# Two stacked cross-attention models: the order of five engines written out by a clock kept while the program is traced

## The chip, the cores and the metric

The kernel runs on one core of one Trainium2 chip. The metric is device time in microseconds (us) of one launch. The kernel before took 2897.28 us, the median of 3 runs (2894.77 to 2900.27).

## The reference

Inputs are `x` and `ctx`, both 16 sequences of 256 tokens of 512 channels, and a mask of 16x256x256. Two model blocks follow each other. In short:

```python
# block 0
q = layer_norm(x) @ q_w;  k, v = split(layer_norm(ctx) @ kv_w)     # 16 heads of 32
x = x + softmax(where(mask, -max, q k^T / sqrt(32))) v @ proj_w + proj_b
x = x + gelu(layer_norm(x) @ fc1_w + fc1_b) @ fc2_w + fc2_b        # 512 -> 2048 -> 512
# block 1, with m = (row of x is not all zero)
x = ln1(x + mha(x, x, Wq1, Wk1, Wv1, m, causal=True))
m = (row of x is not all zero)
x = ln2(x + mha(x, ctx, Wq2, Wk2, Wv2, m, causal=False))
x = ln3(x + (relu(x @ fc1 + b1) @ fc2 + b2) * m)
# mha multiplies Q, K, V and its output by m, counts the non-zero energies of
# query 0 per head ("lengths"), and masks the keys beyond that count
```

Everything is float32. A product is made of three passes of a reduced float32 type: each operand is split into a high part and a low remainder, and high*high, high*low and low*high are added.

## The kernel before

The 16 sequences are handled in 8 groups of two (512 tokens, four tiles of 128 rows, `G = 4`). There are four stages:

1. Block 0's attention, a group at a time (8 groups).
2. Block 0's MLP (`Mlp0.run`), 8 groups of 16 hidden chunks, `up` and `down` alternating.
3. Block 1: 8 self-attention groups, then 8 cross-attention groups (`block1`, the jobs `Mha`).
4. Block 1's MLP (`mlp_feed`), 8 groups.

In the attention stages two generators are interleaved by `weave`. The main one, `Attention.stream`, goes through heads (32 to a group): `scores` (two matmuls on TensorE into one of two `sc` banks of PSUM, the row maximum on VectorE, two exponentials on ScalarE with their sums), three heads later `turn` (transposes of the exponentials into a `pt` bank, and a copy of it to SBUF on ScalarE), and for every eight heads `mix` and `finish`. The other, `feed(g)`, makes the next group's operands meanwhile: it transposes the rows (`transposed`), projects Q, K and V (12 passes of 512 columns for each of 4 chunks), splits each product into its high and low part (`split`: ScalarE makes the high part, VectorE the low), and in block 0 adds the output projection (`residual`). The parts of Q and K go through DRAM (`keep`) and come back as `stack` tiles, three of which exist; `build` loads one for every four heads, with four or five DMAs.

In block 1, `front(n + 1, t)` transposes tile `t` of the next group's rows, and tests them with `nonzero`: a pass over the row on VectorE, whose result is `m`. The rows come by `rows_in`, one DMA into one of three `x` tiles, called when the third Q chunk of group `n` has been projected. That tile is free once `norm` of group `n-2` has stored its rows.

Weights are loaded in rows of 128x512 by `Weight.load`: a DMA, the high part, the low part. In attention they use the nine buffers `pts` that also hold the transposed exponentials; in `Mlp0` four buffers in turn.

The order within an engine is set in two ways. TensorE takes the order in which the program is traced:

```python
    with tc.manual_schedule(engines={mybir.EngineType.PE}):
        block1(phase1())
```

VectorE, ScalarE, GpSimdE and the queue of SyncE, which issues every DMA, are ordered by a planner, which lays out a timeline of its own and may put any instruction that it holds for ready ahead of others. Work of which the tracer knows that it isn't ready is deferred by counting heads: `Attention.later` holds closures, of which one is run after each head.

Of the kernel before, what the change touches and what calls it, by code (L numbers as in the profile page):

```python
# [10 lines left out]
F32 = mybir.dt.float32  # L11
# [9 lines left out]
P = 128  # L21
# [16 lines left out]
PASS = 216.0  # L38
# [5 lines left out]
def kernel(ctx: ExitStack, tc: tile.TileContext, a, out):  # L44

# [58 lines left out]

    def rows(ap):
        return ap.rearrange("(t p) c -> p t c", p=P)
# [16 lines left out]
    def split(src, dst, bias=None, scale=None):  # L123

        if bias is not None:
            nc.scalar.activation(dst[0], src, AF.Identity, bias=bias)
            nc.vector.scalar_tensor_tensor(
                dst[1], src, bias, dst[0].bitcast(F32), ALU.add, ALU.subtract
            )
        elif scale is not None:  # L130
            nc.scalar.activation(dst[0], src, AF.Copy, scale=scale)
            nc.vector.scalar_tensor_tensor(
                dst[1], src, scale, dst[0].bitcast(F32), ALU.mult, ALU.subtract
            )
        else:
            nc.scalar.copy(dst[0], src)
            nc.vector.tensor_tensor(dst[1], src, dst[0].bitcast(F32), ALU.subtract)
# [5 lines left out]
    class Weight:  # L143
# [4 lines left out]
        def __init__(  # L148
            self,
            pool,  # L150
            stage,
# [11 lines left out]
            self.stage = stage  # L163
# [4 lines left out]
            self.form, self.raw = form, {}  # L168
# [8 lines left out]
        def load(self, ks, x0=0, n=C):  # L177

            at = slice(x0, x0 + n)
            for k in ks:  # L180
                h, l = (self.reorder(w[:, k, at]) for w in self.w)
                raw = self.stage()
                nc.sync.dma_start(
                    out=raw, in_=a[self.name][ts(k, P), self.c0 + x0 : self.c0 + x0 + n]
                )
                raw = self.raw[k] = self.order(raw)
                if self.gain is None:
                    nc.scalar.copy(h, raw)
                    nc.gpsimd.tensor_tensor(out=l, in0=raw, in1=h.bitcast(F32), op=ALU.subtract)
                elif self.form is None:  # L190
                    by = self.gain[:, k : k + 1]
                    nc.gpsimd.tensor_scalar(raw, raw, by, None, ALU.mult)
                    nc.vector.tensor_copy(h, raw)
                    nc.gpsimd.tensor_tensor(out=l, in0=raw, in1=h.bitcast(F32), op=ALU.subtract)
                else:
                    by = self.gain[:, k : k + 1]
                    nc.scalar.activation(h, raw, AF.Identity, scale=by)
                    parts = [(l, raw, h)]
                    if self.heads:
                        parts = [(l[:, c], raw[:, c], h[:, c]) for c in range(n // P)]  # L200
                    for to, of, less in parts:
                        nc.vector.scalar_tensor_tensor(
                            to, of, by, less.bitcast(F32), ALU.mult, ALU.subtract
                        )
        def weigh(self, pool):

            self.by_k = None
            for k, raw in self.raw.items():
                self.by_k = weigh(pool, self.by_k, raw, self.offset[:, k : k + 1], self.reorder)

        def shift(self):
# [4 lines left out]
            else:  # L216
                sum_cols(self.b, by_k)

    def load_weight(*args, **kwargs):
        w = Weight(*args, **kwargs)  # L220
        w.load(range(KC))
        return w
# [11 lines left out]
    def sum_cols(b, by_k, first=True):  # L234

        ps = bank("mm", "ps_b")
# [8 lines left out]
    def ln_stats(pool, src):  # L245

        st = pool.tile([P, nc.vector.BN_STATS_DIM], F32, tag="bnst", name="st")
        mv = pool.tile([P, nc.vector.BN_AGGR_DIM], F32, tag="bnmv", name="mv", bufs=4)
        nc.vector.bn_stats(st, src)  # L249
        nc.vector.bn_aggr(mv, st)  # L250
        rstd = pool.tile([P, 2], F32, tag="bnrs", name="rstd", bufs=4)
# [4 lines left out]
    def normalize(pool, dst, src):  # L256
        mean, rstd = ln_stats(pool, src)
        nc.vector.tensor_scalar(dst, src, mean, rstd, ALU.subtract, ALU.mult)

    def layer_norm(pool, x, gain, offset, pooled=False):  # L260
        mean, rstd = ln_stats(pool, x)
        if pooled:
            nc.vector.tensor_scalar(x, x, mean, rstd, ALU.subtract, ALU.mult)
            nc.gpsimd.tensor_tensor(out=x, in0=x, in1=gain, op=ALU.mult)
            nc.gpsimd.tensor_tensor(out=x, in0=x, in1=offset, op=ALU.add)
        else:
            nc.vector.scalar_tensor_tensor(x, x, mean, gain, ALU.subtract, ALU.mult)
            nc.vector.scalar_tensor_tensor(x, x, rstd, offset, ALU.mult, ALU.add)
# [18 lines left out]
    def transposed(dst, src, t, tag="mm"):  # L287
# [4 lines left out]
        split(ps, (dst[0][:, :, ts(t, P)], dst[1][:, :, ts(t, P)]))  # L292
# [55 lines left out]
    def weave(main, n_main, fill, n_fill):  # L348
        a = f = 0.0
        main_on = fill_on = True  # L350
        while main_on or fill_on:
            if fill_on and (not main_on or f * n_main < a * n_fill):
# [5 lines left out]
                if cost is not None:  # L358
                    f += cost
                    continue  # L360
                assert main_on
# [7 lines left out]
            else:  # L369
                a += cost  # L370


    class Attention:
# [8 lines left out]
        def __init__(self, pool, scratch, n, biased):  # L382
# [7 lines left out]
            self.n_build = 0  # L390
            self.later = []
# [948 lines left out]
```

## Time and profile before

| | us |
|---|---|
| median of 3 runs | 2897.28 |
| profiled execution, its own time | 2894.72 |
| its span, first to last instruction | 2892.9 |
| TensorE busy | 2722.3 (94% of the span) |
| VectorE, ScalarE, GpSimdE busy | 1713.3, 1624.5, 777.2 |

So 1.8 us of the profiled execution lie outside its span, and it stands 2.6 us under the median.

The stages, cut in the timeline at the first scores of the groups named. "Clock" is the mean clock that TensorE was granted, as a share of the full one:

| stretch, us from the start | what | length | TensorE busy | VectorE | ScalarE | clock |
|---|---|---|---|---|---|---|
| 0 to 69.4 | group 0's operands, no attention | 69.4 | 43.1 | 52.0 | 36.1 | 0.98 |
| 69.4 to 152.5 | block 0, group 0 | 83.1 | 75.8 | 50.3 | 62.0 | 0.98 |
| 324.3 to 408.0 | block 0, group 3 | 83.7 | 82.0 | 53.1 | 61.3 | 1.00 |
| 652.0 to 730.7 | block 0, last group, and the loading of `fc1_w` | 78.7 | 69.1 | 55.6 | 57.6 | 0.91 |
| 730.7 to 1462.6 | MLP of block 0 | 731.9 | 721.0 | 246.3 | 120.3 | 1.00 |
| 1462.6 to 1501.2 | block 1, group 0's operands | 38.6 | 33.7 | 31.4 | 14.1 | 0.96 |
| 1709.0 to 1781.2 | block 1, a self-attention group | 72.2 | 66.3 | 51.2 | 52.8 | 0.95 |
| 2000.0 to 2079.6 | the last self group, first cross weights | 79.6 | 70.6 | 55.9 | 61.7 | 0.96 |
| 2396.9 to 2476.4 | block 1, a cross-attention group | 79.5 | 73.6 | 52.3 | 59.5 | 0.98 |
| 2636.2 to 2892.9 | last cross group, MLP of block 1 | 256.7 | 237.9 | 188.9 | 112.0 | 0.98 |

The profile's busy time of TensorE counts the modelled tail of a matmul, so a busy TensorE is not one at its peak; how dense the matmuls lie is read from the distance of their starts.

### The profile page before, as it was taken

The page shows a single profiled execution, that of the slowest core. Times are in us where ns is not written, and L with a number is a line of the kernel's source. Part 1 is how long each engine was busy: PE and PEld are TensorE (multiplying, and loading weights), DVE is VectorE, ACT ScalarE, POOL GpSimd, SP SyncE. Part 2 cuts the span into 40 slices and gives each one's busy share as a digit, 9 for nine tenths or more (in the row PEclk, how much of TensorE's full clock was granted, in tenths as well). Part 3 has the DMA queues.
Part 4 walks back from the last instruction along what each step waited for, and adds up shares of the span by engine and source line. Part 5 has one row for each costly group of instructions (what it writes and reads, how often), then busy time and mean ns, then how long its engine had stood idle before and what let it go on. Part 6 is the DMA issues. An engine that isn't in the chain of part 4 may idle for free.

```text
span 2892.9 us, 49424 instructions
## 1 busy us (share of the span) xinstructions
PE 2722.3 (94%) x16698; PEld 2202.6 (76%) x16698; DVE 1713.3 (59%) x5151; ACT 1624.5 (56%) x4732; POOL 777.2 (27%) x714
## 2 busy tenths in 40 slices
PE   6999999998999999999999999998999999998998
PEld 4777778786888888888878777776777777777777
DVE  7666666657533223332267677666766666666777
ACT  5777777777221111111147777777777777777532
POOL 5222212216621001110022222224323332333433
PEclk9999999999999999999999999999999999999999
DMA  7666656656310000000065565556665555654221
GB/s 224 182 170 191 185 167 188 194 168 161 91 44 30 15 15 30 30 30 0 30 212 166 176 176 176 176 176 212 187 194 178 180 169 175 184 179 141 81 102 59
DMA packets 230299, 393.60 MB, mean 136 GB/s; under 512 B 27936, under 2 KB 126752, under 8 KB 230048
## 3 DMA queue, kind: packets, MB, share of 16 engines
q1 hardware_dynamic: 230048, 390.45, 45.0%
q8 instruction: 134, 2.20, 0.3%
q14 instruction: 117, 0.96, 0.1%
HBM read 247.22 MB, written 143.13 MB: 135 GB/s over the span
## 4 chain that ended last, share of the span: by engine, by line
PE 69%; DVE 11%; DMA 10%; ACT 3%; POOL 2%; issue 2%; SPq 1%; POOLq 0%; DVEq 0%; ACTq 0%
PE ps_p L274 26%; PE acc L274 12%; PE ps_v L274 12%; PE ps_pt L465 7%; PE ps_z L482 5%; PE ps_s L424 4%; DMA x<-xd 4%; PE ps_t L291 2%; ACT e L449 2%; DVE e L439 2%; DMA xd<-x 2%; DVE st L249 1%; DVE mn L435 1%; DMA xin<-in_ctx_dram 1%; DVE junk L941 1%
## 5 line engine op out<-in xcount | busy, mean ns | idle before, releaser
L449 ACT ACTIVATE e<-e,mn 128x256 f32<-128x256 f32 (+1 forms) x1024 | 487.3, 480 | 119.0 <-DVE mn L439 115.0
L468 ACT COPY pt<-ps_pt 128x512 f32<-128x512 f32 (+1 forms) x768 | 417.9, 552 | 102.5 <-PE ps_pt L465 98.7
L465 PE MATMUL ps_pt<-ident,e 128*128 128x128 f32 x2816 | 447.7, 278 | 21.5 <-ACT pt L468 19.9
L424 PE MATMUL ps_s<-stack 97*128 97x256 f32 (+1 forms) x1536 | 335.0, 300 | 86.9 <-DVE mn L439 44.3
L875 ACT ACTIVATE hg<-ps_p,b_fc 128x512 f32<-128x512 f32 x128 | 88.1, 688 | 580.5 <-PE ps_p L274 550.0
L465 PEld LDWEIGHTS ps_pt<-ident,e 128*128 128x128 f32 x2816 | 342.1, 143 | 71.9 <-ACT pt L468 34.3
L424 PEld LDWEIGHTS ps_s<-stack 97*128 97x128 f32 (+1 forms) x1536 | 276.1, 193 | 157.2 <-ACT e L449 56.4
L274 PE MATMUL acc<-fc_w_h,hid 128*128 128x512 f32 x1024 | 337.6, 392 | 0.0
L274 PE MATMUL ps_p<-x_t,fc_w_h 128*128 128x512 f32 x1024 | 317.0, 390 | 0.0
L140 DVE CAST hid<-hg 128x512 fp32r<-128x512 f32 x128 | 62.9, 491 | 386.5 <-ACT hg L875 386.4
L253 POOL TENSOR_TENSOR rstd<-rstd,nhalf 128x1 f32<-128x1 f32 x192 | 125.1, 657 | 572.8 <-DVE rstd L252 540.6
L449 ACT ACTIVATE e<-ps_s,mn 128x256 f32<-128x256 f32 x512 | 243.7, 495 | 33.3 <-DVE mn L435 30.7
L439 DVE CUSTOM_DVE_ANT_0 e<-mb,ps_s 128x256 f32<-128x256 bf16 x512 | 190.7, 412 | 73.9 <-PE ps_s L424 70.8
L435 DVE TENSOR_REDUCE mn<-ps_s 128x2 f32<-128x512 f32 x256 | 174.6, 682 | 99.7 <-PE ps_s L424 96.2
L274 PEld LDWEIGHTS acc<-fc_w_h,hid 128*128 128x128 f32 x1024 | 192.3, 188 | 42.2
L274 PEld LDWEIGHTS ps_p<-x_t,fc_w_h 128*128 128x128 f32 x1024 | 192.3, 188 | 42.0
L274 PE MATMUL ps_p<-x_t,q_h 128*128 128x512 f32 x640 | 212.4, 413 | 0.0
L1041 POOL TENSOR_TENSOR x<-x,zz 128x512 f32<-128x512 f32 x64 | 83.6, 1306 | 467.3 <-DVE zz L1034 327.7
L439 DVE CUSTOM_DVE_ANT_0 e<-tri,ps_s 128x128 f32<-128x128 f32 (+1 forms) x512 | 159.9, 345 | 75.7 <-PE ps_s L424 70.7
L274 PE MATMUL ps_p<-x_t,fc_w_l 128*128 128x512 f32 x512 | 201.1, 393 | 0.0
L274 PE MATMUL acc<-fc_w_l,hid 128*128 128x512 f32 x512 | 200.5, 392 | 0.0
L449 ACT ACTIVATION_READ_ACCUMULATOR e<-e,mn 128x1 f32 x1024 | 197.2, 193 | 0.0
(178 smaller groups left out, 5794.6 us busy)
## 6 DMA issues: line engine op xcount, KB each, us to landing
d<-qk SPq DMA_DIRECT2D x192, 512.0 KB
stack<-d SPq DMA_DIRECT2D x384, 256.0 KB
stack<-d SPq DMA_DIRECT2D x384, 128.0 KB
xd<-x SPq DMA_DIRECT2D x96, 256.0 KB
x<-xd SPq DMA_DIRECT2D x24, 1024.0 KB
wst<-in_fc_w_dram SPq DMA_DIRECT2D x48, 256.0 KB
xin<-in_ctx_dram SPq DMA_DIRECT2D x32, 256.0 KB
xr<-in_x_dram SPq DMA_DIRECT2D x32, 256.0 KB
```

Of the source, the lines that this page charges most:

```text
L140: nc.vector.tensor_copy(dst[0], src)
L253: nc.gpsimd.tensor_tensor(out=rstd[:, 1:2], in0=rstd[:, 0:1], in1=nhalf, op=ALU.pow)
L274: nc.tensor.matmul(ps, w[p], x[q], start=(k == 0 and i == 0), stop=(k == kc - 1 and i == 2))
L424: nc.tensor.matmul(ps[:, t, :], st[: self.rows, 0, j % HPC, ts(t, P)], st[: self.rows, 1, j % HPC, :], start=True, stop=True,)
L435: nc.vector.tensor_reduce(mn, ps, AX.X, ALU.min)
L439: nc.vector.tensor_tensor_reduce(out=e[:, at], in0=bias[t], in1=ps[:, t, : job.width[t]], scale=-SC, scalar=BIG, op0=ALU.add, op1=ALU.min, ...
L449: nc.scalar.activation(e[:, at], ps[:, t, :] if bias is None else e[:, at], AF.Exp, bias=mn[:, t : t + 1], scale=-1.0, accum_out=u.rs[:, t ...
L465: nc.tensor.transpose(pp[:, ts(x, P)], e[:, at : at + P], ident)
L468: nc.scalar.copy(pt[:, :n], pp[:, :n])
L482: nc.tensor.matmul(z[ts(j, D), c * S + w[0] * P : (c + 1) * S], job.v[u.i * NT + mc][:, at : at + D], u.pt[c * HPC + j][:, x0 * P : (x0 + ...
L875: nc.scalar.activation(hg, ps, AF.Gelu, bias=b_fc1[:, k : k + 1], scale=1.0)
L1041: nc.gpsimd.tensor_tensor(out=xv, in0=xv, in1=zz, op=ALU.add)
```

## The change

All five engines take the order of the trace (`tc.manual_schedule()` without a list), so no planner moves anything. For that the tracer keeps a clock: `weave` advances it by the price of each traced product (`tick`), and `after(ns, do)` defers a piece of work by that many ns of it. `step_on` runs the next deferred piece at once, `settle` all that are left, and `Loader.ensure(n)` as many as it takes until n weight rows are in.

With that clock, work is placed as follows.

- `split`, `normalize`, `norm`, `residual`, `lengths`, `keep` and the stores: each step that waits for another engine is traced 0.8 to 6 us after it.
- `scores` is divided; the exponentials of head n are traced behind the `turn` of head n-3.
- `build` is called up to two stacks ahead, on heads that don't begin a stack; where none is there when the head needs it, it is called at that head.
- `shared`: in block 0's last group the copy of every second head's transposes goes from ScalarE to VectorE; in cross-attention that of every fourth.
- `nonzero` is a maximum of absolute values and a comparison. It is made where the rows are produced (`Mlp0.out`, and `norm` once stored), not where they are read back.
- `rows_in` (through `next_rows`) comes after the fourth Q chunk, once `norm` of group n-2 has been traced.
- `Loader` replaces `Weight.load`: four rows ahead in block 0, two buffers for `fc1_w`, one buffer (`wst`) for `fc2_w` and for all weights of block 1. Of `fc1_w` ScalarE makes every high part; the low part is VectorE's for even rows, and two GpSimdE instructions for odd ones.
- In `Mlp0` the next group's rows come by one DMA instead of four and are normalized in hidden chunks 5 to 11; their four normalized tiles have a buffer each.
- Pacing prices change (`PASS` 216 to 230 ns, `mix` 1950 to 2100).

The core of the diff:

```diff
+    def after(ns, do, lasting=False):
+        heapq.heappush(due, (now[0] + ns, next(number), lasting, do))
+    def tick(ns):
+        end = now[0] + ns
+        while due and due[0][0] <= end:
+            at, _, _, do = heapq.heappop(due)
+            now[0] = max(now[0], at)
+            do()
+        now[0] = end
...
-    def split(src, dst, bias=None, scale=None):
+    def split(src, dst, bias=None, scale=None, lag=800.0, then=None):
...
+        if lag:
+            after(lag, rest)
...
+    class Loader:
+        def pump(self):
+            while self.queue and self.flying < self.ahead:
+                w, k, x0, then = self.queue.pop(0)
+                raw = self.stage()
+                w.fetch(raw, k, x0)
+                self.flying += 1
+                self.last = max(self.last + self.gap, now[0] + self.wait)
+                after(
+                    self.last - now[0],
+                    lambda w=w, raw=raw, k=k, x0=x0, then=then: self.split(w, raw, k, x0, then),
+                    True,
+                )
+        def split(self, w, raw, k, x0, then):
+            w.use(raw, k, x0)
+            after(750.0, self.landed, True)
+        def ensure(self, n):
+            while self.done < n:
+                step_on()
...
     def stream(self, jobs):
...
                     if j % HPC == 0:
-                        u = units[un]
-                        u.st[j // HPC] = self.build(u.job, u.i, u.c + j // HPC)
-                    self.scores(units[un], j)
-                    yield 2 * 110.0
+                        while n_built <= m:
+                            assert self.build(n_built, jobs)
+                            n_built += 1
+                        u.st[j // HPC] = self.stacks.pop(m)
+                    self.scores(u, j)
+                    if (
+                        n_built <= min(m + len(self.tiles) - 1, len(heads) // HPC - 1)
+                        and n % HPC
+                        and self.build(n_built, jobs)
+                    ):
+                        n_built += 1
+                    yield 2 * 119.0
                 if LAG <= n < len(heads) + LAG:
                     un, j = heads[n - LAG]
                     yield self.turn(units[un], j)
+                if n < len(heads):
+                    self.exponentials(*((units[heads[n][0]], heads[n][1])))
...
-                if self.later:
-                    self.later.pop(0)()
...
     def last():
             yield from more_values(NG - 1)
+            settle()
...
+            mlp.load_up()
...
         def load_up(self):
+            self.up_loader = Loader(self.stage, 2, 3500.0, 1600.0)
             for x0 in range(0, HID, C):
                 for k in range(KC):
-                    self.fc1.load([k], x0)
-                    yield 2 * PASS
+                    self.up_loader.ask(self.fc1, k, x0)
...
     def run(self, early, following, after_up):
+            loader = self.loader = Loader(
+                lambda: pool.tile([P, C], F32, tag="wst", name="wst", bufs=1), 1, 3000.0, 1400.0
+            )
+            for k in range(self.NH):
+                loader.ask(self.fc2, k)
...
     def nonzero(pool, src, m):
-        junk = pool.tile([P, C], F32, tag="t512", name="junk", bufs=3)
-        nc.vector.tensor_scalar(
-            junk, src, 0.0, None, ALU.not_equal, ALU.max, accum_out=m
-        )
+        top = pool.tile([P, 1], F32, tag="top", name="top", bufs=1)
+        nc.vector.tensor_reduce(top, src, AX.X, ALU.max, apply_absolute_value=True)
+        nc.vector.tensor_scalar(m, top, 0.0, None, ALU.not_equal)
...
     def norm(self, t):
+                def stored():
+                    nc.sync.dma_start(
+                        out=xd[3 if self.cross else 2][self.g][ts(t, P), :], in_=x
+                    )
+                    if not self.cross:
+                        nonzero(pool, x, m1[:, self.g, t : t + 1])
+                    self.stored += 1
...
     def front(n, t):
-            cost = transposed(job.x_t, x, t)
-            if n:
-                nonzero(pool, x, job.m[:, t : t + 1])
-            return cost
+            return transposed(job.x_t, x, t, "mm" if t or n else "z")
...
     def feed(n):
-                if c == 2:
-                    next_rows(n)
+            while n >= 2 and jobs[n - 2].stored < G:
+                yield None
+            next_rows(n)
...
-    with tc.manual_schedule(engines={mybir.EngineType.PE}):
+    with tc.manual_schedule():
```

## The prediction

> **What bounds the kernel now.** I read the page's busy shares first, then the waits of TensorE, the timeline about the longest of them, and the chain for the pace of matmuls.
>
> ```profile
> PE 2722.3 (94%) x16698; PEld 2202.6 (76%) x16698; DVE 1713.3 (59%) x5151; ACT 1624.5 (56%) x4732; POOL 777.2 (27%) x714
> ...
> PE ps_s L424 <- DVE mn L439: 44.3, 17, 5.9
> PE ps_s L424 <- ACT e L449: 33.5, 21, 4.6
> ...
> DVE junk L941 <- DMA x<-xd: 46.8, 13, 6.1
> ```
>
> TensorE is the bound, and no other engine is near 94%. It idles 171 us in all. Its longest waits (total, times, longest) are for a row maximum or an exponential, because there are two `sc` banks. The third line says why those are late: VectorE itself stood 13 times, 46.8 us, before `nonzero` (`junk`) for rows still on their way. The timeline of a self-attention group:
>
> ```profile
> 1594.49 0.37 SPq L1062 DMA_DIRECT2D x<-xd  x1
> ...
> 1601.94 0.69 DVE L941 TENSOR_SCALAR_CACHE_REDUCE junk<-x 128x512 f32<-128x512 f32 x1 [5.62 <-DMA x<-xd]
> ...
> 1604.26 0.40 ACT L449 ACTIVATE e<-e,mn 128x128 f32<-128x128 f32 x1 [5.05 <-DVE mn L439]
> ...
> 1604.66 0.76 PE L424 MATMUL ps_s<-stack 97*128 97x256 f32 x2 [5.43 <-DVE mn L439]
> ```
>
> The rows are asked for at 1594.49; VectorE, in order, is stuck behind the test until 1601.94, then does the tests, and the scores wait 5.43 us. This comes once in each later group of block 1.
>
> How dense can it be? The chain (start, length, what) gives 12 passes of 512 columns; the timeline of block 0, two scores and four transposes, by the distance of starts:
>
> ```profile
> 852.71 2.75 PE acc L274 x12
> ...
> 442.54 0.40 PE L424 MATMUL ps_s<-stack 96*128 96x256 f32 x2
> 442.78 0.60 PE L465 MATMUL ps_pt<-ident,e 128*128 128x128 f32 x4
> 443.13 0.71 PE L274 MATMUL ps_p<-x_t,q_w_h 128*128 128x512 f32 x2
> ```
>
> So 0.23 us a pass, 0.12 a score, 0.09 a transpose; a `mix` is 1.6 by the same reading. A self group is 144 passes (33.1), 64 scores (7.7), 96+32 transposes (11.3), 4 mixes (6.4) and 16 matmuls of `lengths` (1.9): 60.3 us, where 72.2 are spent. A cross group is 66.0 against 79.5, a full block 0 group 75.5 against 83.7. Of the 11.9 us of the self group 5.9 are idle (72.2 less 66.3) and 3.6 are the clock (0.95 granted); 2.4 are seams between unlike matmuls, which stay. Of the cross group's 13.5: 5.9 idle, 1.6 clock, 6 seams. Block 0 loses 1.7 idle of its 8.
>
> **What the Trainium skill says.** "TensorE: Matmul & The Clock Gate", Part 1: about 3.4 us of idleness halve the clock until it has been busy as long. The trace agrees: 0.50 from 1605 to 1609 us, after the 5.43 us gap. A stall costs more than itself. "PSUM — Partial Sum Buffer", Engine vs sequencer instructions: ScalarE's, VectorE's and GpSimdE's queues are strict FIFO; the stall above is that. [...]A quiet load here took 2.68 (`wst`, issued 812.51, read 815.19); in attention 3 to 6. "SBUF — State Buffer", two separate sides: a VectorE instruction of two SBUF inputs and GpSimdE exclude each other. The low part of `hid` took 0.69 alone and 1.66 beside GpSimdE: agrees, and no forecast rests on more.
>
> **The change, part by part.** In the instruction order of the changed kernel TensorE has the same 15,135 instructions, SyncE 24 fewer, VectorE 136 more, ScalarE 64 fewer. So no product gets cheaper; all depends on waits.
>
> *Tests and rows, block 1.* Removed are 64 tests of 0.68+0.08; added are 64 maxima (nearest row: `mn` of 128x512, 0.68) and comparisons (nearest 0.13): +3 us of VectorE, beside other work, as VectorE has 21 us free in a self group. They now read rows in SBUF and wait for no load. Bounds: -10 to +15 us. Gone is the 5.4 us gap with its half clock. Late next is TensorE itself: its first transposes of the rows. By the order, 5.7 us of TensorE work lie between the load's issue and them in self groups, 8.8 in cross groups; the load takes 6.6 to 7.5 us (self) and 6.0 to 6.6 (cross) in the chain. So 1.3 us come back per self group, none in cross. Six self groups regain 5.9+3.6-1.3 = 8.2, less 1 for a lost head or so (ScalarE has 19 us free, in order): **-43**. Six cross groups: 5.9+1.6-1 = 6.5: **-39**. The two at the seam of self and cross idle 9.0 and 5.0; new loads (below) use half: **-8**.
>
> *`shared`.* 80 copies of 0.57 go from ScalarE to VectorE (nearest 0.68): both keep over a quarter free. Nothing; without that cover at most 0.1 a head.
>
> *One-buffer loaders.* A row's cycle is load, ScalarE's high part, GpSimdE's low part, next issue. For `fc2_w`: 2.7+0.6+1.45+0.2 = 4.9 us, where the clock grants 3.75. Sixteen rows in ScalarE's queue fall behind the order by 1.15 each; behind row 14 stands gelu 11, and behind that `down` and TensorE. Of 16 us two chunks of slack (11) absorb most: +8 (0 to 16). For block 1 the cycle is 4.3+1.2+1.6+0.3 = 7.4 against 4.75, so each set of four rows blocks ScalarE 3 x 2.6 = 8 us, of which perhaps 3 are absorbed. Sets k1, v1 at block 1's start: +8; q2, k2, v2: in the seam's -8; f1, f2: +7. The first stacks of each attention have nothing ahead of them: `build` issues four DMAs of 0.5 when the first scores are next, and these land 4 to 5 us later: +6 in block 0, +6 in block 1.
>
> *`fc1_w`.* The odd rows share one buffer: 3.0 (load) + 0.6 + 1.56+1.29 (GpSimdE) + 0.4 = 6.9 us each; seven intervals take 48 us, where the order puts 25 us of TensorE's work. ScalarE, and SyncE with the stacks behind it, wait. 55 of dense work and 2 of seams become 80, against 78.7 now, since GpSimdE's two steps for all 16 rows (3 us each) pace it already: +2 (-12 to +12).
>
> *Start.* TensorE idles 26 us of the first 69.4: 7.5 before the first tile, 6.4 before the second, whose normalization stood behind other tiles. Tile after tile costs about 3.2 us of VectorE and ScalarE; I take **-11** (-18 to 0).
>
> *Block 0.* Row loads have 4 to 5 us of work ahead of them, where 23 waits for them stalled VectorE 40 us. Against that five heads run without passes beside them, while `residual` waits for `done`; they were three: ScalarE needs 1.7 a head, TensorE 0.6, so +1.5 a group. Net **-9** (-20 to +5).
>
> *MLP of block 0.* The fronts' waits (0.37 and 1.11 at seven groups) go, as the tiles are ready four chunks early: -10. *MLP of block 1:* the load of the next rows stands in SyncE's queue behind the last output store of the group before, and has 6 us for 5 to 6: +3 (0 to 10).
>
> Sum: -43-39-8-11-9-10+8+8+7+6+6+2+3 = **-80**, and -20 for the short waits elsewhere (33 us of excess in the last stretch, 16 in block 0's first group): **-100**. 2894.7-100 = 2794.7; the median stands 2.6 above: I say 2796.
>
> **Rivals.** *All is regained*: loads land early enough for ScalarE never to meet one unlanded. Then the loaders' +23 and half the +12 fall away, and cross and self lose nothing: 2740. For it: quiet loads of 2.7 us. Against: one buffer.
> *The wait changes its owner*: TensorE stands for the rows itself as long as VectorE did. Then only half of 82 in block 1 comes: 2840. For it: 5.7 against 7 us.
> *ScalarE becomes the bound, slower.* Place: the self and cross groups. Strict trace order puts head n's exponentials behind head n-3's copy, and that behind TensorE. In a dense self group ScalarE has (65-52.8)/32 = 0.38 us a head to wait in, in a cross group (72.5-57)/32 = 0.48. Each 0.1 beyond costs 0.1 x 32 x 16 = 51 us. From about 0.65 a head it eats the 100. At 0.75 the time is 2960. For it: no planner fills a gap. Against: `turn` precedes scores whose exponentials are due 4.4 us later (two banks).
> *The change doesn't do what it says*: the order shows that it does, on every engine.
>
> **How the numbers follow.** Likeliest 2796, its own range 2745 to 2835, chance 0.55; all regained 0.13; owner changed 0.15; no change to speak of 0.03; slower 0.14. 0.2% is 6 us, about what a measurement can tell. Faster 0.83. Range 2735 to 2875, which leaves out the slower case and a little below.
>
> **What would show it.** Right: no VectorE wait for `x<-xd` in block 1, self groups of 64 to 66 us and cross of 72 to 74 at a clock of 1.00, ScalarE waiting for `wst`, TensorE once for `stack` at each start. Wrong: self groups at 72 with ScalarE or TensorE waiting elsewhere, or the `fc1_w` stretch over 95.

## The result, and the profile after

The changed kernel took 3013.91 us, the median of 4 runs (3007.41 to 3017.12), against 2896.52 us for the kernel before: 1.040 of its time, 95% interval 1.038 to 1.042. The forecast was 2796 us (2735 to 2875), with a chance of 0.14 for slower. The profiled execution spans 3015.3 us, 122.4 more than before.

The page and the waits of TensorE (in all, times, longest, in us) of the changed kernel:

```profile
PE 2769.2 (92%) x16698; PEld 2219.0 (74%) x16698; DVE 1831.7 (61%) x5223; ACT 1589.0 (53%) x4668; POOL 744.4 (25%) x698
```

```profile
PE ps_s L517 <- ACT e L547: 52.0, 69, 3.2
PE ps_t L374 <- DMA x<-xd: 25.2, 8, 12.3
...
PE ps_s L517 <- DMA stack<-d: 14.8, 2, 9.0
...
PE ps_t L374 <- DVE wst L346: 9.5, 1, 9.5
PE ps_p L357 <- DVE tok L1131: 7.9, 1, 7.9
```

VectorE no longer waits for `x<-xd` anywhere, as forecast. But TensorE, still the busiest engine at 92%, now idles 246 us instead of 171, for many different things: rows, stacks, a normalized tile, the first-token row. It is also busy 47 us longer with the same products. The clock that it was granted is 0.970 on the mean, where it was 0.981; by an estimate from these two figures that is 35 us of the 122.

Cut at the first scores of each group, as in the table of before, the time went here (lengths in us; the last two columns are experiments told below):

| stretch | before | forecast, as a difference | after | difference | `planner4` | `before_tests` |
|---|---|---|---|---|---|---|
| start | 69.4 | -5 | 93.5 | +24.1 | 77.6 | 69.4 |
| block 0, first seven groups | 582.7 | -9 | 599.2 | +16.5 | 576.7 | 578.6 |
| last group and `fc1_w` | 78.7 | +2 | 94.8 | +16.1 | 79.8 | 76.6 |
| MLP of block 0 | 731.9 | -2 | 729.6 | -2.3 | 742.9 | 732.5 |
| block 1: operands and first group | 101.1 | +14 | 118.9 | +17.8 | 107.3 | 109.6 |
| six self groups | 436.3 | -43 | 420.2 | -16.1 | 411.8 | 416.2 |
| seam, two groups | 157.0 | -8 | 155.6 | -1.4 | 148.7 | 148.7 |
| six cross groups | 479.2 | -32 | 497.0 | +17.8 | 466.6 | 450.0 |
| last cross group, MLP of block 1 | 256.8 | +3 | 306.5 | +49.7 | 268.2 | 256.5 |

(The -20 that the forecast gave to "short waits elsewhere" belongs to no row.) A steady self group and a steady cross group of the kernel after, by windows (length, then busy time and instructions of TensorE, its weight loads, VectorE, ScalarE and GpSimdE, then TensorE's clock, DMA share and GB/s):

```profile
1704.30:1772.40 68.10, 64.92 (x481) 53.33 (x480) 52.50 (x219) 51.48 (x181) 17.62 (x17) 1.00 0.63 187
...
2374.60:2456.60 82.00, 75.89 (x528) 59.47 (x528) 57.22 (x128) 55.76 (x177) 23.91 (x20) 0.98 0.57 170
```

The self group has its clock back (1.00, 0.95 before) and is 4 us shorter. The cross group is longer than before (79.5), with the same work on TensorE.

Where a cross group waits, the timeline shows. Each line: start, length, engine and line; in brackets the idle time before it and what ended it.

```profile
2475.14 0.68 DVE L174 SCALAR_TENSOR_TENSOR qk<-ps_p,qk 128x512 fp32r<-128x512 f32 x1
...
2475.44 0.51 PE L517 MATMUL ps_s<-stack 97*128 97x256 f32 x2
2475.74 0.68 DVE L176 TENSOR_TENSOR c_t<-ps_t,c_t 128x512 fp32r<-128x512 f32 x1
...
2476.34 0.68 DVE L335 BATCH_NORM_STATS2 st<-x 128x6 f32<-128x512 f32 x1
...
2477.34 0.68 DVE L528 TENSOR_REDUCE mn<-ps_s 128x2 f32<-128x512 f32 x1
...
2478.12 0.47 ACT L547 ACTIVATE e<-ps_s,mn 128x256 f32<-128x256 f32 x1 [2.25 <-DVE mn L528]
...
2479.19 0.80 PE L517 MATMUL ps_s<-stack 97*128 97x256 f32 x2 [2.10 <-ACT e L547]
```

The scores of 2475.44 are done by 2475.95, but their row maximum starts at 2477.34: VectorE has two low parts and the statistics of a norm ahead of it, which the clock of traced products placed there. ScalarE waits 2.25 us for that maximum, and TensorE 2.10 us for ScalarE to free a bank. The same wait of 2.1 us stands in each of the six cross groups of the table.

In the MLP of block 1 a group takes 30.3 us (fronts at 2875.15 and 2905.41), where its 96 passes and 16 transposes are 23.5 at the forecast's prices and a group of the kernel before took 24.2:

```profile
2823.65 0.74 DVE L1482 SCALAR_TENSOR_TENSOR x<-x,mv,ln 128x512 f32<-128x512 f32 x1
2823.73 1.82 POOL L1473 TENSOR_TENSOR x<-x,y 128x512 f32<-128x512 f32 x1
...
2824.49 1.60 DVE L1485 SCALAR_TENSOR_TENSOR x<-x,rstd,ln 128x512 f32<-128x512 f32 x1
...
2826.12 14.52 SPq L1486 DMA_DIRECT2D out_dram<-x  x4
...
2840.75 0.38 SPq L1453 DMA_DIRECT2D x<-xd  x1
2846.27 0.63 PE L374 MATMUL ps_t<-ident,x 128*128 128x128 f32 x4 [1.73 <-DMA x<-xd]
```

VectorE's last pass over a tile takes 1.60 us, beside GpSimdE's addition of 1.82. The four output stores leave SyncE between 2826.12 and 2840.6, each when VectorE is done with its tile, and the load of the next rows stands behind the last of them. It is issued at 2840.75, lands 5.5 us later, and TensorE has waited 1.73 us.

### The profile page after: what moved, and what is told of

Its sections match the earlier page's. It is cut to its first block, busy times and chain, and to the rows that moved or that the text cites. A ratio compares the mean times of both kernels' runs of the same rounds, so it can differ in the third digit from the quotient of the medians.

```text
span 3015.3 us, 49215 instructions
## 1 busy us (share of the span) xinstructions
PE 2769.2 (92%) x16698; PEld 2219.0 (74%) x16698; DVE 1831.7 (61%) x5223; ACT 1589.0 (53%) x4668; POOL 744.4 (25%) x698
## 4 chain that ended last, share of the span: by engine, by line
PE 62%; DVE 17%; DMA 6%; ACT 6%; issue 4%; POOL 4%; SPq 0%; POOLq 0%; DVEq 0%; ACTq 0%
PE ps_p L357 23%; PE acc L357 11%; PE ps_v L357 10%; PE ps_pt L562 6%; PE ps_z L583 4%; PE ps_s L517 4%; DMA wst<-in_fc_w_dram 3%; ACT e L547 3%; PE ps_t L374 2%; DVE st L335 2%; DMA x<-xd 2%; DVE mn L528 2%; DVE x L1485 1%; DVE e L531 1%; DVE x_t L176 1%
## 5 line engine op out<-in xcount | busy, mean ns | idle before, releaser
L547 ACT ACTIVATE e<-e,mn 128x256 f32<-128x256 f32 (+1 forms) x1024 | 487.4, 481 | 77.3 <-DVE mn L531 76.5
L569 ACT COPY pt<-ps_pt 128x512 f32<-128x512 f32 (+1 forms) x688 | 372.2, 541 | 157.2 <-PE ps_pt L562 156.2
L339 POOL TENSOR_TENSOR rstd<-rstd,nhalf 128x1 f32<-128x1 f32 x192 | 113.4, 591 | 953.8 <-DVE rstd L338 940.8
L357 PE MATMUL ps_p<-x_t,q_h 128*128 128x512 f32 x640 | 219.1, 422 | 15.5 <-DVE tok L1131 7.9
```

The lines of the kernel that those rows point to most:

```text
L339: nc.gpsimd.tensor_tensor(out=rstd[:, 1:2], in0=rstd[:, 0:1], in1=nhalf, op=ALU.pow)
L357: nc.tensor.matmul(ps, w[p], x[q], start=(k == 0 and i == 0), stop=(k == kc - 1 and i == 2))
L547: nc.scalar.activation(e[:, at], e[:, at] if ps is None else ps[:, t, :], AF.Exp, bias=mn[:, t : t + 1], scale=-1.0, accum_out=u.rs[:, t, ...
L569: nc.scalar.copy(pt[:, :n], pp[:, :n])
```

## The experiments

Each ratio below is against runs of the kernel before made beside it, with its 95% interval. Lengths of stretches come from the profile of each. Those of the four kernels that free one engine, and of the mended ones, are to be read against the 3014 us of the changed kernel.

### Is it the order, or the edits?

`planner4` leaves every edit and gives four engines back to the planner.

```diff
-    with tc.manual_schedule():
+    with tc.manual_schedule(engines={mybir.EngineType.PE}):
```

> The changed kernel with the order of the trace for TensorE alone; VectorE, ScalarE, GpSimdE and SyncE are ordered by the planner again, every edit and every placement stays. Theory A (the strict order of the four other engines costs the time, the edits do not): the start falls from 93.5 to about 70 us, the fc1_w stretch from 94.8 to about 80, the last stretch from 306 to about 260, cross groups from 82 to 79, self groups stay near 68; sum 2865 to 2900 us. Theory B (the edits cost it: one-buffer loaders, GpSimdE's low parts, late first stacks): within 25 us of the changed kernel's 3014.

Measured: 2880.31 us, 0.9934 (0.9908 to 0.9960). So the strict order of VectorE, ScalarE, GpSimdE and SyncE costs some 133 us, and the rest of the change gains 0.7%. The table shows where: 15.9 us in the start, 22.5 in block 0, 15.0 at `fc1_w`, 30.4 in the cross groups, 38.3 in the last stretch. In block 0's MLP alone the strict order is 13.3 us better; there the planner had put high parts on ScalarE ahead of their loads (`fc_w_h` waited for `wst` 16 times, 64.0 us in all; once 6.21 us, at 760.04).

`sync_free`, `vector_free`, `scalar_free` and `gpsimd_free` each give back one engine. For VectorE:

```diff
-    with tc.manual_schedule():
+    with tc.manual_schedule(engines={PE, Activation, Pool, SP})   # each of mybir.EngineType
```

> The changed kernel with only SyncE's queue given back to the planner; the four compute engines keep the order of the trace. Theory A1 (loads stand behind stores in SyncE's queue): the last stretch loses its 2 us wait for rows in each of seven groups and the 12 us one, 306 to about 275 us, the two waits for first stacks (9.0 and 5.7) shrink by half, in all 2965 to 2985. Theory A2 (VectorE and ScalarE, in order, are what is late, and SyncE only waits for them): over 3000.

> The changed kernel with VectorE alone given back to the planner; TensorE, ScalarE, GpSimdE and SyncE keep the order of the trace. Theory V (in the cross groups VectorE's bulk work, placed by the clock, stands in a clump of 4 us ahead of the row maxima that the next scores need): cross groups fall from 82 to about 77 us, and the last stretch from 306 to about 285, since the norms of two tiles can overlap again; sum 2930 to 2965. Theory S (ScalarE's order, my rival before the result): cross groups stay at 81 to 82, sum over 2990.

> The changed kernel with ScalarE alone given back to the planner. Theory V: cross groups stay at 81 to 82, only stretches with weight loading gain (start, fc1_w, group 448), sum 2975 to 3000. Theory S: cross groups fall to 77, sum under 2965.

> The changed kernel with GpSimdE alone given back to the planner. Theory P (in the fc1_w stretch a norm's rstd stands behind two GpSimdE steps of a weight row, and at block 1's start the clearing of tok behind a row's low part): the fc1_w stretch falls from 94.8 to 82 to 87, block 1's start from 54.0 to 46 to 49, the rest as before; sum 2985 to 2998. Other theory (GpSimdE only follows the others): both unchanged, sum over 3005.

| freed | us | ratio (interval) | start | `fc1_w` | steady cross group | last stretch |
|---|---|---|---|---|---|---|
| none (after) | 3013.91 | 1.040 (1.038 to 1.042) | 93.5 | 94.8 | 82.0 | 306.5 |
| VectorE | 2954.02 | 1.021 (1.019 to 1.023) | 89.5 | 92.3 | 77.2 | 286.9 |
| SyncE | 2965.67 | 1.023 (1.020 to 1.026) | 84.3 | 96.8 | 81.6 | 279.1 |
| GpSimdE | 2987.06 | 1.032 (1.030 to 1.034) | 93.6 | 96.3 | 80.4 | 282.9 |
| ScalarE | 2992.49 | 1.034 (1.032 to 1.037) | 89.0 | 98.4 | 80.0 | 304.9 |
| all four | 2880.31 | 0.993 (0.991 to 0.996) | 77.6 | 79.8 | 76.5 | 268.2 |

("Steady" is the mean of the groups that begin at heads 608 to 672.) In the cross groups VectorE's order is the largest cause: it alone gives back 4.8 us, where all four give 5.5. ScalarE alone gives 2.0, more than expected (81 to 82 us), and GpSimdE 1.6, so the gains overlap. The window of such a group in `vector_free`, with the columns of the windows above:

```profile
2352.70:2430.00 77.30, 73.12 (x529) 58.19 (x529) 57.86 (x128) 55.99 (x177) 23.83 (x20) 1.00 0.60 178
```

The busy times of VectorE and ScalarE are those of the kernel after within about 1% (57.22 and 55.76 there), so the engines do the same work; only the order on VectorE is free, and the clock is whole (1.00, 0.98 there). The wait for the first stack, 9.0 us, is SyncE's order. The first stack's first part, in the kernel after and in `sync_free`:

```profile
86.56 0.51 SPq L504 DMA_DIRECT2D stack<-d  x1
```

```profile
72.92 0.54 SPq L504 DMA_DIRECT2D stack<-d  x1
```

In the strict order it is asked for behind everything traced earlier; with SyncE free the wait is gone. The last stretch is shortened by freeing any of VectorE, SyncE and GpSimdE, by 20 to 27 us each, 72 with ScalarE's 1.6, where all four together give 38: the same time is gained in more than one way. In the whole the four gains add up to 156 us against 133 by the medians, or to 145 against 135 by the ratios; the runs of the kernel before that stood beside them differ by up to 6 us, so only a part of this excess is sure. My expectation for GpSimdE was wrong in both places that it named (`fc1_w` 96.3, block 1's start 54.5); its gain lay in the last stretch, and 9 us of it in the six cross groups. That the sum fell into the expected range was luck.

### The row tests alone

`before_tests` is the kernel before, with its planner, and one part of the change: the test as a maximum and a comparison, where rows are made.

```diff
 def norm(self, t):
     nc.sync.dma_start(out=xd[3 if self.cross else 2][self.g][ts(t, P), :], in_=x)
+    if not self.cross:
+        nonzero(pool, x, m1[:, self.g, t : t + 1])
 def front(n, t):
-    cost = transposed(job.x_t, x, t)
-    if n:
-        nonzero(pool, x, job.m[:, t : t + 1])
-    return cost
+    return transposed(job.x_t, x, t)
```

(and likewise at the end of block 0's MLP)

> The kernel before with one part of the change: the row test (as a maximum and a comparison) is made where the rows are produced, and not where they are read back. The planner stays. If the prediction's step for block 1 holds (VectorE's wait for the rows is what costs 5.9 us idle and the half clock in each group), self groups fall from 72.5 to about 67 and cross groups from 79.5 to about 75, in all 2835 to 2865. If another wait takes its place, 2885 to 2900.

Measured: 2839.56 us, 0.980 (0.9778 to 0.9822). A self and a cross group of it:

```profile
1701.90:1769.40 67.50, 65.54 (x482) 53.50 (x481) 51.51 (x221) 52.49 (x180) 18.02 (x16) 1.00 0.63 189
2279.30:2352.80 73.50, 71.86 (x528) 58.59 (x528) 51.60 (x121) 59.05 (x185) 24.01 (x20) 1.00 0.64 188
```

A self group falls from 72.2 to 67.5, a cross group from 79.5 to 73.5, with a clock of 1.00 in both. TensorE idles 2.0 and 1.6 us in them instead of 5.9. This part of the change gives about two thirds of what the forecast gave it, and is the only large gain in the change: the other edits take 41 us of it back (2880 against 2840) and the strict order 133 more. It has costs of its own: block 1's operands and first group take 109.6 us instead of 101.1, and the group at head 448 takes 77.9 instead of 72.2, since TensorE now stands 8.8 us behind the loading of the first cross weights. In the first case the reason isn't settled.

### The last stretch, step by step

Three kernels, each with one more edit, all five engines in the order of the trace. (`adds_apart` also drops the deferral of the addition by 3 us, and puts TensorE's transposes of the next tile behind the products of the present one. In `tail_no_wait` the rows of group 3, which do need it, wait for the last cross group.)

```diff
# rows_early: group g+2 asked for in group g
+    if t == 2 and 1 <= g and g + 2 < NG:
+        mrows(g + 2)
     yield from down(g, t)
# adds_apart: GpSimdE's addition to tile t+1, traced ahead of the norm of tile t
     ps = yield from project(w["k"].w, h_ts[g], t)
+    yield mfront(g + 1, t + 1)
+    added(g + 1, t + 1, y)
# tail_no_wait: group 2's rows don't wait for the last cross group
-    while jobs[-2 if g == 0 else -1].stored < G:
+    while g == 0 and jobs[-2].stored < G:
         yield None
...
+        while g == 1 and jobs[-1].stored < G:    # ahead of mrows(g + 2)
+            yield None
```

> The changed kernel, with the rows of MLP group g+2 of block 1 asked for ahead of the third down tile of group g, so that they no longer stand in SyncE's queue behind the output stores of group g-1's and g's tail. Theory A1 (SyncE's queue): TensorE's wait of 2.1 us for x<-xd and its half clock (1.7 us) go in five of seven groups, the period falls from 30.3 to about 27, in all 20 us less than the changed kernel. Theory A2 (VectorE is the bound there, at 4.8 us a tile): the period stays above 29 and the wait moves to the x_t split; under 6 us less.

> The kernel of rows_early, and in block 1's MLP GpSimdE's addition to the next tile is traced ahead of the norm of the present one, so that it runs beside VectorE's reading of PSUM and not beside its last pass over x. Theory (VectorE is the bound of the last stretch at 4.8 us a tile, of which 0.9 us is that pass taking 1.65 instead of 0.74 us beside GpSimdE): the pass takes 0.75 again, the period of a group falls from 28 to about 25, the last stretch from 289 to 265 to 272. Other theory (the wait for GpSimdE's rstd paces it): the period stays at 28.

> The kernel of adds_apart, and the rows of MLP group 2 no longer wait, in the trace, for the last cross group to be stored (their tile doesn't need it; only those of group 3 do). Theory (the 12 us gap of TensorE in the last stretch is a chain of norm, store, load, made by that place in SyncE's queue): the gap goes, the last stretch falls from 284 to about 268, which is what the planner has with the same edits (268.2). Other theory (those rows are late for another reason, the last norm itself): the gap moves to group 3 and the stretch stays above 278.

| kernel | us | ratio (interval) | period of an MLP group | last stretch |
|---|---|---|---|---|
| after | 3013.91 | 1.040 (1.038 to 1.042) | 30.3 | 306.5 |
| `rows_early` | 2999.08 | 1.035 (1.032 to 1.037) | 26.5 | 288.8 |
| `adds_apart` | 2989.55 | 1.033 (1.031 to 1.036) | 25.7 | 284.0 |
| `tail_no_wait` | 2973.19 | 1.027 (1.026 to 1.029) | 25.7 | 266.3 |

The queue of SyncE costs 3.8 us a group, as expected (3 or more); in the whole it is 15 us, not 20. Taking GpSimdE's addition away from VectorE's last pass gives 0.8 a group, less than expected, and in the whole the two intervals overlap. The pass is 0.94 us now (mean of 14, by groups of instructions in adds_apart) where it was 1.65 (of 16, in after):

```profile
L1485 DVE SCALAR_TENSOR_TENSOR x<-x,rstd,ln 128x512 f32<-128x512 f32 x16 | 26.4, 1649 | 3.0 <-POOL rstd L339 1.8
```

```profile
L1496 DVE SCALAR_TENSOR_TENSOR x<-x,rstd,ln 128x512 f32<-128x512 f32 x14 | 13.2, 944 | 2.8 <-POOL rstd L339 1.8
```

The 12 us gap came from one line, which waited for rows that another tile needs; without it the stretch is as short as the planner's (268.2). So most of the loss here was placement, and placement can mend it; the last 10 us to the 256.8 of the kernel before are not found, and a group still takes 25.7 us where it took 24.2.

### The other stretches

`no_shared_copy` and `planner4_no_shared` give every copy of cross-attention back to ScalarE, in the strict and in the planned order:

```diff
     def shared(self, j):
-        return self.cross and j % HPC == 3
+        return False
```

> The changed kernel, in cross-attention with every copy of transposes on ScalarE again (VectorE makes none): 5.4 us of VectorE less in each group, 4.6 of ScalarE more. Theory V (VectorE's clump ahead of a row maximum is what the scores wait for): cross groups fall from 82 to about 80. Theory that the clump is made of norms and first tokens alone: unchanged within 0.5 us. Theory S (ScalarE): 83 to 84.

> The kernel of planner4 without VectorE's copies in cross-attention. If `shared` is what the edits cost there (76.5 us a cross group against 73.8 with the row tests alone): cross groups about 74, sum 12 to 18 less than planner4. If something else (the exponentials traced behind the turn, TensorE's order): within 5 us of planner4.

Measured: 3003.03 us, 1.0376 (1.0349 to 1.0404), with steady cross groups of 80.2; and 2864.72 us, 0.9898 (0.9884 to 0.9913), with 76.1. In the strict order VectorE's copies cost 1.8 us in a steady cross group, so "nothing" was wrong for them; but they are the smaller part of the loss there (8 us, the difference between 82.0 and the 73.8 of `before_tests`). In the planned order a steady cross group gains only 0.4, and not the 2.5 that the expectation gave it; the sum came down as expected, mostly in other stretches. In the whole the gains are 11 and 16 us by the medians and 7 and 10 by the ratios, with intervals that overlap those without the edit, so their size is not shown. Why the planned cross group stays 2.3 us above the 73.8 of `before_tests` (the same mean) isn't settled.

`weigh_late` traces the weighing of a weight row behind the high part of the next one. In the changed kernel the two engines call each other (ScalarE, then VectorE, at the start):

```profile
26.89 1.16 ACT L316 ACTIVATE wst<-wst,cvec 128x512 f32<-128x512 f32 x1 [1.88 <-DVE q_w_l L250]
27.96 1.17 ACT L241 ACTIVATE q_w_h<-wst,cvec 128x512 fp32r<-128x512 f32 x1
```

```profile
29.16 1.76 DVE L250 SCALAR_TENSOR_TENSOR q_w_l<-wst,cvec,q_w_h 128x128 fp32r<-128x128 f32 x4 [2.36 <-ACT q_w_h L241]
```

L316 scales the row in place, so it must follow VectorE's reading; the next high part stands behind it on ScalarE, and VectorE waits for that: 4.1 us a row.

```diff
 w.use(raw, k, x0)
-if then is not None:
-    then(raw)
+held, self.held = self.held, then and (lambda: then(raw))
+if held:
+    held()
```

> The changed kernel; in the first loader, the weighing of a weight row (ScalarE scales the row in place, after VectorE has read it for the low part) is traced behind the next row's high part. Theory (a circle of ScalarE, VectorE and ScalarE again, 4.1 us a row, paces the start): a row costs about 2.4 us, the start falls from 93.5 to 78 to 84 us, nothing else moves; sum 10 to 16 less than the changed kernel. Other theory (loads pace the start, one by one): under 4 us less.

Measured: 3006.66 us, 1.0379 (1.0352 to 1.0406); the start is 90.2 us, 3.3 less. The number is that of the other theory (under 4 us), though not for its reason: TensorE's waits for the high parts (`q_w_h`) fell from 6.5 to 2.9 us, so the circle was real and small. The waits for GpSimdE's sums of the weighed rows stayed (7.5 and 8.0 us).

`strict_mended` adds, on top of `tail_no_wait`, `no_shared_copy` and `weigh_late`, three mends:

```diff
-    load("o")
+    after(3000.0, lambda: load("o"))              # proj_w behind the first stacks
-    if self.form is None and k % 2:               # GpSimdE's low parts of fc1_w
-        ...
-    nc.gpsimd.memset(q0.bitcast(F32), 0.0)        # tok
+    nc.vector.memset(q0.bitcast(F32), 0.0)
```

> All five engines in the order of the trace, with mends each in its own stretch: those of tail_no_wait (last stretch), no_shared_copy (cross groups), weigh_late, and three new: the rows of proj_w are asked for behind the first stacks; the low part of every fc1_w row is VectorE's; tok is cleared by VectorE. If the places named are the causes: start 93.5 to about 82, fc1_w stretch 94.8 to 84, block 1's start 54.0 to 47, cross groups 80.3 as in no_shared_copy, last stretch 266; sum 2925 to 2945. If only the planner's freedom can mend them: each new stretch stays within 3 us, sum about 2955 to 2960.

Measured: 2957.78 us, 1.0218 (1.0201 to 1.0235). That is the sum expected if only the planner's freedom can mend the new stretches, and two of the three new mends did little. The start is 89.5 us: the first stack is asked for 3 us sooner (83.43) and TensorE still waits 8.2 us for it. At block 1's start the reason was read rightly in the timeline of after:

```profile
1529.70 2.73 POOL L476 MEMSET stack<- 1x1024 f32 x3
1532.48 0.72 POOL L1306 MEMSET tok<- 128x80 f32 x6
1532.68 0.20 DVE L186 CAST tok<-own 128x16 fp32r<-128x16 f32 x1 [10.55 <-POOL tok L1306]
```

VectorE stood 10.55 us for a clearing of 0.72 us, which stood on GpSimdE behind the low parts of `k`'s rows and the clearing of stacks (2.73 us). Clearing on VectorE cuts TensorE's wait from 7.9 to 3.3 us; but then TensorE waits 4.7 for `lengths` and 2.3 for rows, and the stretch is 53.3 against 54.0. The `fc1_w` stretch fell to 89.9, a third of what the planner gives; no single engine's freedom and no edit tried gave the other 10 us.

### A kernel that beats both

In `before_tests` groups 448, 480 and 704 stay long: the loads of new weights. `tests_two_step` splits a row three heads after asking for it; `tests_rows_first` asks for all four rows at once.

```diff
-    att.later += [lambda k=k: w[x].load([k]) for k in range(KC)]
# tests_two_step: steps[k] asks for row k, steps[k + 3] makes its parts
+    att.later += [lambda s=s: [do() for do in s] for s in steps]
# tests_rows_first: all four asked for here, and the 1 MB of rows after them
+    uses = [u.begin(k) for k in range(KC)]
+    att.later[:0] = [lambda: None] * 2 + uses
```

> The kernel of before_tests (the planner, row tests where rows are made), and in block 1 a weight row that is loaded beside attention is asked for at one head and split three heads later, so that the planner cannot put its high part on ScalarE before the row has landed. Theory (ScalarE stood 5.45 us before such a row in group 448, TensorE 8.8 behind it): groups 448, 480 and 704 fall from 77.9, 74.2 and 80.9 to about 70, 71 and 76; sum 2820 to 2832. Other theory (bandwidth of the loads themselves, or the buffers that the rows share with the exponentials): 2836 to 2850.

> The kernel of before_tests; in block 1 the four rows of each new weight are asked for at once, those of q ahead of the 1 MB load of the next group's rows, and split one a head from the third head on. Theory (the rows landed 8.5 us after their issue since the 1 MB load went first, and ScalarE stood 5.3 us before the first): group 448 falls from 77.9 to about 71, 704 from 80.9 to about 77, sum 2826 to 2833. Other theory (any weight load in these groups costs its share of a full DMA): within 3 us of 2838.

Measured: 2836.43 us, 0.9801 (0.9787 to 0.9816), and 2839.76 us, 0.9814 (0.9798 to 0.9829): the same as the tests alone, with groups 448 of 78.1 and 79.9 us. The timeline of `tests_two_step` shows what is left:

```profile
1936.04 0.37 SPq L1076 DMA_DIRECT2D x<-xd  x1
...
1937.05 0.45 SPq L180 DMA_DIRECT2D wst<-in_w_q_dram  x1
...
1945.54 1.07 ACT L184 CAST q_h<-wst 128x512 fp32r<-128x512 f32 x1 [5.27 <-DMA wst<-in_w_q_dram]
```

ScalarE's step stands behind a load that hasn't landed: it starts 8.5 us after the row was asked for, just behind the 1 MB of `x` rows. Whether those rows are what delays it isn't shown. `tests_rows_first` was to test it, but tracing the weight rows first did not move them ahead of `x` in the planner's queue (`x` is asked for at 1934.72, the first weight row at 1935.73). No run tells these three kernels apart. The kernel before with the row tests moved is the simplest of them, 2.0% under the kernel before (interval 1.8 to 2.2%).

## Why the prediction was wrong

**The tests' step was right in mechanism, and two thirds in size.** Forecast for moving them: -43 in six self groups, -39 in six cross groups, -8 at the seam. Alone they gave -20.1, -29.2 and -8.3. The five steady cross groups gained 5.8 us each of 6.5, the five steady self groups 5.2 of the 7.2 that were left after a lost head. In these self groups TensorE's idle time fell by 3.8, about as summed (5.9 less 1.3 and 1), but its busy time by 1.3 only, where the sum gave 3.6 to the clock: that term was mis-sized. The wait for rows, "1.3 us come back per self group", did not happen; no steady self group after the change shows one. The remaining difference is in two groups with weight loads: 448, which got longer (77.9, 72.2 before), and 704, which kept its length (80.9).

**The step that failed is the one without a term.** The sum priced moves, buffers and loads, and let four engines go from a planner to a fixed order for nothing, except where a loader blocks ScalarE. The runs price it at 133 us. VectorE has 30% of its time free in a steady cross group (57.22 of 82.00 us are busy), and yet its order costs up to 4.8 us there. The timeline shows how: the clock that places its bulk work knows the price of products and not how full VectorE's queue is, and three items stand ahead of a row maximum. That this clump is the whole of the 4.8 us isn't shown.

**The other edits were mis-sized too.** Beside the tests the sum had +10 for them and -20 for short waits elsewhere. In the planner's order they cost 41 us (`planner4` against `before_tests`): 16.6 in the six cross groups, 11.7 in the last stretch, 10.4 in block 0's MLP, 8.2 in the start. They were written for the strict order, and no run takes these 41 us apart further than VectorE's copies.

**"MLP of block 1: +3 (0 to 10)" was the largest mis-sized term**: +49.7. The mechanism was named, a row load behind an output store, and it was worth 17.7 us of the stretch (`rows_early`). Not named were a traced wait for the last cross group, again 17.7 (`tail_no_wait`), and the pass of VectorE that takes 1.65 us beside GpSimdE, of which "no forecast rests on more" was said: 4.8 with the other moves of `adds_apart`. Some 10 us remain open.

**Start: -11, and +6 for the first stacks; measured +24.1.** The wait of 6.4 us was read as that before the second tile; it stood before the third. In the kernel before, the first two tiles were transposed together:

```profile
7.46 1.97 PE L291 MATMUL ps_t<-ident,wst 128*128 128x128 f32 x8 [7.46 <-DVE wst L258]
15.80 1.12 PE L291 MATMUL ps_t<-ident,wst 128*128 128x128 f32 x4 [6.37 <-DVE wst L258]
```

In the kernel after, the four tiles come at 5.95, 9.93, 13.90 and 16.97, the last one only 0.6 us sooner than before (17.58). So the -11 had little under it. Of the 24.1 us lost, SyncE's order is worth 9.2 (`sync_free`), the circle of ScalarE and VectorE in the loader's rows 3.3 (`weigh_late`), and 8.2 stay when the planner orders all four engines. The stack was +9.0, not +6.

**Block 0: -9, measured +16.5** in its first seven groups, nearly all of it in the first four (88 to 90 us each). There TensorE waits 8.9 us, four times, for GpSimdE's sums of weighed `fc1_w` rows (`by_k`) and 8.7 us for ScalarE's copies, which had no term. Freeing ScalarE alone gives 9.4 back, GpSimdE 6.1, SyncE 5.2, VectorE nothing, all four 22.5; the cause is not taken further apart.

**`fc1_w`: +2, measured +16.1.** The cycle of a row was worked out, but not that the norm of the MLP's first tile stands behind it on GpSimdE and VectorE: TensorE waits 9.5 us for `wst` L346. With VectorE's low parts for every row that wait is still 6.4 (`strict_mended`), so its full cause stays open.

**Block 1's start: +14, measured +15.4 before the first scores and +2.4 in the first group.** The size came out, by another way: the loaders' blocking of ScalarE was forecast, while the largest wait, 7.9 us, came from a clearing on GpSimdE, with others close behind it. And half of it, 8.5 us, comes with the row tests alone (`before_tests`). So the near value was luck. **Block 0's MLP: -2, measured -2.3.** Both terms show: TensorE's waits at the fronts (10.9 us before) are gone, and 6.1 us of new waits came for the loader's and the hidden chunks' parts.

**The rivals.** The slower one had the right sign, and by chance a value (2960) that is nearer than the likeliest one. But its place and its engine were wrong in the main: ScalarE freed alone gives 0.6 to 0.7%, 2.0 us in a steady cross group, and a steady self group lost 0.2 us (68.2, and 68.0 in `planner4`). The chance of 0.14 for slower was too low. The forecast had shown that all gain lay in waits, and a fixed order makes waits on every queue; that deserved a case of its own with VectorE and SyncE in it.

## What to carry to other kernels

Fixing the order of an engine is a change with its own price, even of an engine with 30% of its time free: for each instruction that the critical engine waits for, read which bulk work the new order puts directly ahead of it. Take from a large rewrite the one part whose wait the profile shows, and try it alone; here that part, a test moved to where its data is in SBUF, kept 2% that the rest turned into a loss of 4%. A queue of DMAs in order makes a load as late as the store ahead of it, so ask when that store's data is ready, not only how long the load takes.

## What was not expected of the hardware

A VectorE pass of 128x512 with two SBUF inputs took 1.65 us on the mean when a GpSimdE addition had started before it, and 0.74 for the same kind of instruction (L1482) that starts before the addition. The Trainium skill, "SBUF — State Buffer", two separate sides, says that one of the two blocks the other for the whole instruction; this trace agrees, and shows the GpSimdE instruction lengthened too (1.64 us on the mean in the MLP groups of after, 1.33 in those of `adds_apart`).

TensorE's clock halved after waits shorter than the 3.4 us that "TensorE: Matmul & The Clock Gate", Part 1, gives: after the 2.10 us gap in the cross group the window that follows (2479.1 to 2482.3 us, below) has a clock of 0.50, the third number from the end. It was so in five of six cross groups with this gap. The measurement decides: a wait of about 2 us can already be followed by a half clock. It need not be: the sixth of these gaps (it ends at 2234.41), and one of 2.19 us in `before_tests` (it ends at 242.92), left the clock whole. What it costs is at most some 1.6 us (half of 3.2, an estimate); in the self groups, where 3.6 us went to the clock by its mean, the busy time fell by only 1.3 when the clock was whole again.

```profile
2479.10:2482.30 3.20, 3.11 (x11) 2.71 (x12) 2.26 (x9) 1.58 (x7) 2.70 (x3) 0.50 0.70 205
```
